# A 7x7 convolution beside attention: rows by six products for four outputs in place of four for two

## The chip, the cores and the metric

The program runs on one core of a Trainium2 chip. The metric is the device time of one execution in microseconds (us). The core has TensorE (PE, with its weight loads PEld), VectorE (DVE), ScalarE (ACT) and GpSimd (POOL) for the work, and SyncE (SP), whose queue issues the DMAs.

## The reference

There are three stages over four images x of 128 channels and 64x64 points. Only the first is touched here, called layer 0:

```python
def _L0_conv_ref(x, w7, b7, w5, b5, w3, b3, gw, gb, tw, tb, pw, pb, ow, ob):
    x7 = conv2d(x, w7, b7, 3)
    x5 = conv2d(x, w5, b5, 2)
    x3 = conv2d(x, w3, b3, 1)
    xn = nonlocal_block(x, gw, gb, tw, tb, pw, pb, ow, ob)
    return jax.nn.relu(x7 + x5 + x3 + xn + x)
...
x = x + _L0_conv_ref(_gn(x), ...)
```

`_gn` is a group norm. The three convolutions have the same input, so they are one 7x7 convolution with the summed kernel, 128 channels to 128. `nonlocal_block` is softmax attention over the 4096 points of an image, with 64-wide theta, phi and g, an output projection and a residual. Then follow a two-way selective state-space layer (`mamba`) and a recurrence over time (`recurrence`), both over the same `t`.

## The kernel before

All four images lie in SBUF as `t`, 128 channels by 4 x 4096. Layer 0 goes in 32 steps, eight per image. Each step does the attention of one block of 512 queries and one part of the convolution. The order of PE's instructions is the order of the code; on the other engines a scheduler orders them when the program is built, and each engine then keeps that order.

The attention of a step (`scores`, `values`): 16 times, two matmuls of 512 columns give scores `pf` in PSUM (two buffers), ACT takes the exponential `ex` (four buffers, L393), two matmuls multiply by `gT` and add to `acc`, and DVE sums the exponentials into `es` (L408). `divide` inverts the sums; `finish` projects.

The convolution divides the seven kernel rows into rows 0 to 2, row 3 and rows 4 to 6. Rows go by four products for two outputs (m = 0 to 3), and the two groups of three rows by three products in place of four (n = 0, 1, 2: both groups' sum, then each). Columns are treated the same way (kx = 0 to 3). An image is cut into two bands of 32 rows, held as the padded copies `xps[0]` and `xps[1]`; the four steps of a band are m = 1, 2, 0, 3. Per step:

- `forms(p, m)`: POOL makes `yx` (a combination of two rows, one buffer), `yd` (its differences, one buffer), and from them the column combinations `yf` (four buffers), each four instructions of 272 elements per partition.
- `convolve(p, i)`: for each n SP loads 576 KB of weights `wt` (two buffers) from `wd` in DRAM, and `products` makes 10 matmuls of 256 columns, or 20 where m is 0 or 3 and n is 1 or 2 (kernel row 3 with weights `wc` joins). An ACT copy (L348) and DVE additions bring PSUM into `eo`, POOL adds the n = 0 result (L358). m = 1 is kept as `mid`, m = 2 makes sum and difference with it, and m = 0 and 3 write the band's result `cv` (L372, POOL).

A band's `finish` comes in the first step of the next band: a matmul, an addition into `cv`, Relu with the bias (ACT, L426), and the addition to `t` (POOL, L428). In an image's last step `keys` makes the next image's `phi` and `gT` between the products, and `rows` normalises rows into `xps`. `weights` runs once at the start: it uses the places of images 1 to 3 in `t`, makes the column weights by `thirds` (L447 to L451), then 12 sets of `wd`, with a scaling by -1 on ACT (L467):

```python
for m in ORDER:
    one, two = lots[0][m], lots[1][m]
    both = fm.tile([P, 9, P], F32, tag="wt", name="both")
    nc.gpsimd.tensor_tensor(both, one, two, ALU.add)
    nc.sync.dma_start(wd[3 * m], both)
    nc.sync.dma_start(wd[3 * m + 1], one)
    nc.scalar.mul(two, two, -1.0)
    nc.sync.dma_start(wd[3 * m + 2], two)
```

Images 1 to 3 are loaded after it (`load(n)`), and `statistics` reads each with eight bn_stats.

Of the kernel before, what the change touches and what calls it, by code (L numbers as in the profile page):

```python
# [10 lines left out]
F32 = mybir.dt.float32  # L11
# [5 lines left out]
P = 128  # L17
# [136 lines left out]
def conv_attention(nc, tc, k, a, t, B, H, W, flags, load, mem, loads):  # L154
# [11 lines left out]

    T = H * W
# [4 lines left out]
    QB = 4  # L172
    RB = QB * RW
    PR, PC = RB // 2, W // 2
    KB = PR // 4
# [3 lines left out]
    SLOT = ((0, 1, 7, 2), (4, 5, 8, 6))  # L179

    with ExitStack() as ctx:
# [11 lines left out]
        xps = [wp.tile([P, RB + 6, WP], F32, name=f"xp{i}") for i in range(2)]  # L193
# [13 lines left out]
        for xp in xps:  # L207
            nc.gpsimd.memset(xp, 0.0)
# [3 lines left out]
        wd = [dram.tile([P, 9, P], F32, name=f"wd{i}") for i in range(12)]  # L212
# [60 lines left out]
        def rows(b, p):  # L273

            xp = xps[p % 2]
            first = 3 if p == 0 else 6
            n = min(RB + 6 - first, H - (p * RB + first - 3))
            if p == 0:
                nc.gpsimd.memset(xp[:, 0:3, :], 0.0)
            else:  # L280
                nc.vector.tensor_copy(xp[:, 0:6, :], xps[1 - p % 2][:, RB : RB + 6, :])
            nc.vector.tensor_scalar(
                xp[:, first : first + n, 3 : 3 + W],
                t[:, ds(b * T + (p * RB + first - 3) * W, n * W)].rearrange("p (h w) -> p h w", w=W),
                *gn[b], ALU.subtract, ALU.mult,
            )
            if first + n < RB + 6:
                nc.gpsimd.memset(xp[:, first + n :, :], 0.0)

        def combine(out, at, i):  # L290

            x, y, op = ((0, 2, ALU.subtract), (1, 2, ALU.add), (2, 1, ALU.subtract), (3, 1, ALU.subtract))[i]
            nc.gpsimd.tensor_tensor(out, at(x), at(y), op)  # L293

        def forms(p, m):

            xp = xps[p % 2]  # L300
            yx = fm.tile([P, PR + 2, WP], F32, tag="yx", name="yx", bufs=1)
            combine(yx, lambda j: xp[:, j : j + 2 * PR + 3 : 2, :], m)
            yd = fm.tile([P, PR, WP], F32, tag="yd", name="yd", bufs=1)

            def both(rows, g):
                v = rows.rearrange("p (k g e) c -> p k g e c", g=2, e=2)[:, :, g]
                f = fm.tile([P, 4, KB, 2, PC + 2], F32, tag="yf", name="yf", bufs=4)
                for kx in range(4):
                    combine(f[:, kx], lambda j: v[:, :, :, j : j + 2 * PC + 3 : 2], kx)
                return v, f  # L310

            out = [[both(yx[:, 0:PR], 1)]]
            nc.gpsimd.tensor_tensor(yd, yx[:, 0:PR], yx[:, 2 : PR + 2], ALU.subtract)
            for g in range(2):
                out.append([both(yd, g)])
                if m in (0, 3):
                    out[-1].append(both(xp[:, 3 + m // 3 : 3 + m // 3 + 2 * PR - 1 : 2, :], g))
            return out

        def products(f, kxs):  # L320

            pm = ps_c.tile([P, 2, PR * PC // 2], F32, tag="c", name="pm")
            for e, kx in enumerate(kxs):
                terms = []
                for rows, sums, wt in f:
                    for s in range(2):
                        terms.append((sums[:, kx, :, :, 2 * s : 2 * s + PC], wt[:, SLOT[s][kx], :]))
                    if kx in (0, 3):
                        c = 3 + kx // 3
                        terms.append((rows[:, :, :, c : c + 2 * PC - 1 : 2], wt[:, 3, :]))  # L330
                for i, (src, wt) in enumerate(terms):
                    nc.tensor.matmul(pm[:, e, :], wt, src, start=(i == 0), stop=(i == len(terms) - 1))  # L332
            return pm

        ORDER = (1, 2, 0, 3)

        def convolve(p, i):

            m = ORDER[i]
            base = None  # L340
            for n in range(3):
                wt = fm.tile([P, 9, P], F32, tag="wt", name="wt")
                nc.sync.dma_start(wt, wd[3 * m + n])
                f = [v + (u,) for v, u in zip(fs[p, m][n], (wt, wc))]
                pm = products(f, (1, 2))
                keep = n and m == 1
                eo = wk.tile([P, 2, PR * PC // 2], F32, tag=f"mid{n}" if keep else "eo", name="eo", bufs=1 if keep else 4)
                nc.scalar.copy(eo[:, 1, :], pm[:, 1, :])  # L348
                for e, op in enumerate((ALU.add, ALU.subtract)):
                    nc.vector.tensor_tensor(eo[:, e, :], pm[:, 0, :], eo[:, 1, :], op)  # L350
                yield
                pm = products(f, (0, 3))
                nc.vector.tensor_tensor(eo, eo, pm, ALU.add)  # L353
                if n == 0:
                    base = eo
                    yield
                    continue
                nc.gpsimd.tensor_tensor(eo, eo, base, ALU.add)  # L358
                if m == 1:
                    mid[n] = eo  # L360
                elif m == 2:
                    u = wk.tile([P, 2, PR * PC // 2], F32, tag=f"u{n}", name="u", bufs=1)
                    nc.gpsimd.tensor_tensor(u, mid[n], eo, ALU.add)
                    nc.gpsimd.tensor_tensor(mid[n], mid[n], eo, ALU.subtract)
                    mid[n] = [u, mid[n]]
                else:
                    if m == 0 and n == 1:
                        cv[p] = wk.tile([P, RB, W], F32, tag="cv", name="cv", bufs=1)
                    out = cv[p].rearrange("p (k g e q) (c x) -> p g q x k e c", g=2, e=2, q=2, x=2)[:, n - 1, m // 3]
                    in_ = lambda v: v.rearrange("p x (k e c) -> p x k e c", e=2, c=PC)  # L370
                    for x in range(2):
                        nc.gpsimd.tensor_tensor(out[:, x], in_(mid[n][m // 3])[:, x], in_(eo)[:, x], ALU.add)  # L372
                yield
            fs.pop((p, m))

        def queries(n):
            b, q = divmod(n, NQ)
            pt = ps_c.tile([P, NC], F32, tag="c", name="pt")
            r = 3 + (q % QB) * RW
            nc.tensor.matmul(pt, tw, xps[q // QB % 2][:, r : r + RW, 3 : 3 + W], start=True, stop=True)  # L380
# [29 lines left out]
        def divide(n, acc, es):  # L410
            den = ps_c.tile([P, NC], F32, tag="c", name="den")
            nc.tensor.matmul(den, k.ones, es[:, 0, :], start=True, stop=True)
            att = wk.tile([P, NC], F32, tag="att", name="att", bufs=QB + 1)
# [6 lines left out]
        def finish(n, att):  # L420
            b, q = divmod(n, NQ)
            pc = ps_c.tile([P, NC], F32, tag="c", name="pc")
            nc.tensor.matmul(pc, ow, att, start=True, stop=True)
            r = cv[n // QB][:, ds(q % QB * RW, RW), :].rearrange("p r c -> p (r c)")
            nc.vector.tensor_tensor(r, r, pc, ALU.add)
            nc.scalar.activation(r, r, AF.Relu, bias=bsum)  # L426
            tg = t[:, ds(n * NC, NC)]
            nc.gpsimd.tensor_tensor(tg, tg, r, ALU.add)  # L428

        def weights():  # L430
# [24 lines left out]
            lots = []  # L455
            for i, y in enumerate((0, 4)):
                new = free[:, 9 * (i + 1) : 9 * (i + 2), :]
                thirds([w[:, y + i] for i in range(3)], new)
                lots.append([w[:, y], w[:, y + 1], new, w[:, y + 2]])
            for m in ORDER:  # L460
                one, two = lots[0][m], lots[1][m]
                both = fm.tile([P, 9, P], F32, tag="wt", name="both")
                nc.gpsimd.tensor_tensor(both, one, two, ALU.add)
                nc.sync.dma_start(wd[3 * m], both)
                nc.sync.dma_start(wd[3 * m + 1], one)

                nc.scalar.mul(two, two, -1.0)  # L467
                nc.sync.dma_start(wd[3 * m + 2], two)
# [3 lines left out]
        gn, fs, mid, cv, atts = {}, {}, {}, {}, {}  # L472
        NB = NT // 4
        N = B * NQ
        gn[0] = statistics(0)
        rows(0, 0)
        th = None
        for j in range(T // XT):
# [4 lines left out]
            run(part)  # L483
        nxt = scores(th, 0)
        fm = ctx.enter_context(tc.tile_pool(name="l0_fm", bufs=2))
        weights()
        loads()
        for n in range(N):
            b, q = divmod(n, NQ)
            more = b + 1 < B and q == NQ - 1  # L490
            if 0 < n < B:
                load(n)
            m = ORDER[q % QB]
            fs[n // QB, m] = forms(q // QB, m)
            if b + 1 < B and q == NQ - 3:
                gn[b + 1] = statistics(b + 1)
            if (q + 1) % QB == 0 and n + 1 < N:
                rows(*divmod(n // QB + 1, NQ // QB))
# [9 lines left out]
            for i, _ in enumerate(convolve(n // QB, q % QB)):  # L508
                if i == 0:
                    if q % QB == 0 and n:  # L510
                        for m in range(n - QB, n):
                            finish(m, atts.pop(m))
                        cv.pop(n // QB - 1)
                    atts[n] = divide(n, acc, es)
                if more and i < T // XT:
# [9 lines left out]
                if more and i < T // XT:  # L525
                    run(part)
            if n + 1 < N:
                nxt = scores(th, 0)
        for m in range(N - QB, N):
            finish(m, atts.pop(m))  # L530
# [1066 lines left out]
```

## Time and profile before

| | us |
|---|---|
| three runs, median (lowest to highest) | 3230.27 (3229.05 to 3232.55) |
| the profiled execution, its span | 3233.0 |
| first product of the convolution (`pm`, L332) starts | 86.8 |
| last product of the convolution ends | 1733.7 |
| waits of PE's scores `pf` for ACT's `ex` up to 1740 | 28.5 |

The page gives an engine's busy time as a sum, then its busy share in 40 slices of the span (each digit is tenths), and groups of instructions with count, busy time and mean duration in ns of one, then the idle time before them and who ended it. A matmul in float32 stands as two records. In the timeline, the time in brackets is the engine's idle time before the row and its releaser.

### The profile page before, as it was taken

How to read it: one execution, taken by the hardware profiler on the slowest of the kernel's cores; microseconds unless marked ns; L12 is line 12 of the kernel's file. 1: busy time of each engine (PE TensorE's matmuls, PEld its weight loads, DVE VectorE, ACT ScalarE, POOL GpSimd, SP SyncE). 2: the span in 40 equal slices, each digit the busy share in tenths (PEclk: the TensorE clock that was granted, in tenths of full speed). 3: DMA queues.
4: the chain of work that ended last, by engine and by line, in shares of the span. 5: the costliest groups of instructions: out<-in, count | busy, mean ns of one | idle time of the engine just before them, and what ended most of it. 6: DMA issues, size and time to landing. Idle time of an engine off the chain costs nothing.

```text
span 3233.0 us, 43827 instructions
## 1 busy us (share of the span) xinstructions
PE 3043.7 (94%) x15991; PEld 1554.8 (48%) x15991; DVE 2140.1 (66%) x3431; ACT 1751.5 (54%) x3027; POOL 1796.9 (56%) x1487
## 2 busy tenths in 40 slices
PE   5999999999999999999997899999999999999986
PEld 1454544554545444545454354444444544444545
DVE  6865657667566566565664676767667767677667
ACT  3333333333333333342432787887788778888756
POOL 6565554845465546465472266556655665555554
PEclk8999999999999999999998899999999999999988
DMA  4301100101011010101011334333333343334332
GB/s 171 150 30 37 37 30 30 37 31 36 30 37 37 30 44 23 33 34 44 23 45 58 89 93 118 95 92 92 111 94 101 84 117 92 98 99 96 86 113 106
DMA packets 107245, 226.44 MB, mean 70 GB/s; under 512 B 25550, under 2 KB 29262, under 8 KB 105868
## 3 DMA queue, kind: packets, MB, share of 16 engines
q1 hardware_dynamic: 105804, 222.23, 23.4%
q8 instruction: 128, 2.10, 0.3%
q10 hardware_dynamic: 1216, 1.31, 0.1%
q14 instruction: 97, 0.79, 0.1%
HBM read 206.60 MB, written 16.90 MB: 69 GB/s over the span
## 4 chain that ended last, share of the span: by engine, by line
PE 78%; DVE 6%; POOL 5%; ACT 5%; DMA 3%; issue 2%; SPq 0%; POOLq 0%; ACTq 0%; DVEq 0%
PE pm L332 18%; PE acc L402 14%; PE pf L391 14%; PE pb L946 6%; PE px L958 3%; PE y L1077 3%; PE px L967 2%; PE acc L1419 2%; PE po L1148 2%; PE y L1085 2%; PE ptr L1020 2%; PE small L1055 2%; PE small L1032 1%; PE pm L1125 1%; DMA ct<-csmem 1%
## 5 line engine op out<-in xcount | busy, mean ns | idle before, releaser
L393 ACT ACTIVATE ex<-pf 128x1024 f32<-128x1024 f32 x512 | 496.7, 1021 | 515.8 <-PE pf L391 499.6
L408 DVE TENSOR_TENSOR es<-es,ex 128x1024 f32<-128x1024 f32 x448 | 626.3, 1398 | 160.1 <-ACT ex L393 129.1
L391 PE MATMUL pf<-theta,phi 64*128 64x512 f32 x2048 | 515.1, 622 | 28.9 <-ACT ex L393 28.5
L402 PE MATMUL acc<-ex,gT 128*64 128x512 f32 x2048 | 490.5, 605 | 0.0
L1045 POOL TENSOR_TENSOR ct<-ct,Cst 128x512 f32<-128x512 f32 x128 | 168.4, 1316 | 405.5 <-DMA ct<-csmem 348.4
L332 PE MATMUL pm<-yf,wt 128*128 128x256 f32 x1536 | 384.0, 380 | 0.0
L391 PEld LDWEIGHTS pf<-theta,phi 64*128 64x128 f32 x2048 | 174.6, 187 | 347.1 <-ACT ex L393 226.6
L332 PEld LDWEIGHTS pm<-yf,wt 128*128 128x128 f32 x1536 | 285.7, 189 | 95.3 <-issue 50.9
L1011 ACT ACTIVATE lt<-lt,cs 128x128 f32<-128x128 f32 x1024 | 312.1, 390 | 0.0
L293 POOL TENSOR_TENSOR yf<-yd 128x272 f32<-128x272 f32 x256 | 302.7, 1210 | 1.3
L348 ACT COPY eo<-pm 128x256 f32<-128x256 f32 x96 | 35.7, 372 | 480.3 <-PE pm L332 480.3
L402 PEld LDWEIGHTS acc<-ex,gT 128*64 128x64 f32 x2048 | 127.5, 136 | 337.7 <-issue 328.5
L293 POOL TENSOR_TENSOR yf<-xp 128x272 f32<-128x272 f32 x128 | 141.8, 1133 | 203.2 <-PE pm L332 203.2
L946 PE MATMUL pb<-tl,wbc_fwd 128*64 128x512 f32 x512 | 238.5, 609 | 2.7 <-DVE xT L978 2.5
L946 PE MATMUL pb<-tl,wbc_bwd 128*64 128x512 f32 x512 | 239.1, 609 | 0.0
L293 POOL TENSOR_TENSOR yx<-xp 128x1260 f32<-128x1260 f32 x32 | 84.6, 2645 | 215.5 <-PE pm L332 212.7
L350 DVE TENSOR_TENSOR eo<-pm,eo 128x256 f32<-128x256 f32 x192 | 80.7, 420 | 170.0 <-ACT eo L348 167.3
L353 DVE TENSOR_TENSOR eo<-eo,pm 128x512 f32<-128x512 f32 x96 | 64.2, 669 | 190.5 <-PE pm L332 190.1
L1110 POOL TENSOR_TENSOR yT<-yT,zT 128x512 f32<-128x512 f32 x127 | 168.2, 1333 | 37.9 <-DVE yT L1097 32.7
L1044 DVE TENSOR_TENSOR lt<-lt,gm 128x1024 f32<-128x1024 f32 x128 | 181.3, 1417 | 1.9
L1077 PE MATMUL y<-lt,xdt 128*64 128x128 f32 x2048 | 143.2, 283 | 6.7 <-PE ptr L1020 3.8
L978 DVE SCALAR_TENSOR_TENSOR xT<-px,taps_bwd,xT 128x512 f32<-128x512 f32 x192 | 143.7, 749 | 8.2 <-ACT xT L972 3.3
(274 smaller groups left out, 5607.4 us busy)
## 6 DMA issues: line engine op xcount, KB each, us to landing
lt<-csmem SPq DMA_DIRECT2D x128, 512.0 KB, 5.6
wt<-wd SPq DMA_DIRECT2D x96, 576.0 KB, 3.7
ct<-csmem SPq DMA_DIRECT2D x256, 128.0 KB, 5.3
rs<-m SPq DMA_DIRECT2D x31, 512.0 KB, 3.5
t<-in_x SPq DMA_DIRECT2D x4, 2048.0 KB, 9.4
rows<-after SPq DMA_DIRECT2D x32, 256.0 KB, 4.7
out<-t SPq DMA_DIRECT2D x4, 2048.0 KB, 14.3
tl<-scale SPq DMA_DIRECT2D x24, 256.0 KB, 5.4
```

The source lines that it names most:

```text
L293: nc.gpsimd.tensor_tensor(out, at(x), at(y), op)
L332: nc.tensor.matmul(pm[:, e, :], wt, src, start=(i == 0), stop=(i == len(terms) - 1))
L391: nc.tensor.matmul(pf[:, e, :], phi[HALF[e], m, :], th[HALF[e]], start=True, stop=True)
L393: nc.scalar.activation(ex, pf, AF.Exp, scale=scale)
L402: nc.tensor.matmul(acc[HALF[e]], gT[:, 2 * m + e, :], ex[:, e, :], start=(m == 0), stop=(m == NT // 2 - 1))
L408: nc.vector.tensor_tensor(es, es, ex, ALU.add)
L946: nc.tensor.matmul(out, w[i]["bc"][:, tap, bass.ts(c, DS)], src, start=(tap == 0), stop=(tap == KC - 1),)
L1011: nc.scalar.activation(v, v, AF.Relu, scale=-1.0, bias=m["b"]["cs"][:, d, m["i"], h : h + 1])
L1044: nc.vector.tensor_tensor(lt, lt, gm.unsqueeze(2).to_broadcast([P, ND, NHEAD, P]), ALU.mult)
L1045: nc.gpsimd.tensor_tensor(m["ct"], m["ct"], Cs[:, cols].unsqueeze(1).to_broadcast([P, NHEAD, P]), ALU.mult)
L1077: nc.tensor.matmul(y[HALF[h], d, c, at[d]], m["dt"][:, d, 2 * c + h, :], m["lt"][:, d, 2 * c + h, :], start=(i % 2 == 0 and c == 0), stop= ...
L1110: eng.tensor_tensor(v, v, gr["z"][d][:, :, half(d, j // 2)], ALU.mult)
```

## The change

Rows now go by six products for four outputs, at the points 0, 3/4, 3/2 and their negatives, with row 3's two middle outputs done by themselves (m = 6, 7, weights `wc`). The whole image is one padded copy `xp`, in blocks of four rows; its eight steps are m = 1, 2, 0, 6, 7, 5, 3, 4, in the last image 1, 2, 3, 4, 6, 7, 5, 0. `transform` replaces the one combination of rows by scalings on ACT and additions on POOL, into `yx` and `yb` that have one buffer each. The result is summed in the image's own place in `t`, and the input is read again from DRAM (`xr`) for the last addition, at the first step of the next image. `weights` makes 18 sets, in three parts: before step 0, in step 1 and in step 2; the loads of images 1 to 3 come after that. The core of the diff:

```diff
-            yx = fm.tile([P, PR + 2, WP], F32, tag="yx", name="yx", bufs=1)
-            combine(yx, lambda j: xp[:, j : j + 2 * PR + 3 : 2, :], m)
+            if m in (0, 5):
+                j = m // 5
+                nc.scalar.mul(yx, row(j + 2), -(UU + VV))
+                nc.scalar.mul(yb, row(j), UU * VV)
+                nc.gpsimd.tensor_tensor(yx, yx, row(j + 4), ALU.add)
+                nc.gpsimd.tensor_tensor(yx, yx, yb, ALU.add)
+            elif m in (1, 3):
+                nc.scalar.mul(yb, row(1), -(VV if m == 1 else UU))
+                nc.gpsimd.tensor_tensor(yb, yb, row(3), ALU.add)
+                nc.scalar.mul(yx, row(2), -(VV if m == 1 else UU))
+                nc.gpsimd.tensor_tensor(yx, yx, row(4), ALU.add)
+                nc.scalar.mul(yb, yb, U if m == 1 else V)
+                nc.gpsimd.tensor_tensor(yx, yx, yb, ALU.add)
+            else:
+                nc.scalar.mul(yb, yb, -2.0)
+                nc.gpsimd.tensor_tensor(yx, yx, yb, ALU.add)
...
+            if m >= 6:
+                return [None] + [[both(every(m - 2, KB), g)] for g in range(2)]
...
-                if m == 1:
+                if keep:
                     mid[n] = eo
                 elif m == 2:
-                    u = wk.tile([P, 2, PR * PC // 2], F32, tag=f"u{n}", name="u", bufs=1)
+                    nc.gpsimd.tensor_tensor(out(0), in_(mid[n]), in_(eo), ALU.add)
+                    nc.gpsimd.tensor_tensor(mid[n], mid[n], eo, ALU.subtract)
+                    nc.scalar.mul(out(2), out(0), UU)
+                    nc.scalar.mul(out(1), in_(mid[n]), U)
+                    nc.scalar.mul(out(3), in_(mid[n]), U * UU)
+                elif m == 4:
+                    u = wk.tile([P, 2, KB // 2 * PC], F32, tag="u", name="u", bufs=2)
                     nc.gpsimd.tensor_tensor(u, mid[n], eo, ALU.add)
                     nc.gpsimd.tensor_tensor(mid[n], mid[n], eo, ALU.subtract)
-                    mid[n] = [u, mid[n]]
+                    nc.gpsimd.tensor_tensor(out(0), out(0), in_(u), ALU.add)
+                    for j, v, by in ((2, u, VV), (1, mid[n], V), (3, mid[n], V * VV)):
+                        for x in range(2):
+                            nc.vector.scalar_tensor_tensor(
+                                out(j)[:, x], in_(v)[:, x], by, out(j)[:, x], ALU.mult, ALU.add
+                            )
                 else:
...
+                    j = {0: 0, 5: 3, 6: 1, 7: 2}[m]
+                    nc.gpsimd.tensor_tensor(out(j), out(j), in_(eo), ALU.add)
...
+        def finish(b):
+            for q in range(NQ):
+                xr = wk.tile([P, NC], F32, tag="xr", name="xr")
+                nc.sync.dma_start(xr, image_in(b)[:, bass.ts(q, NC)])
+                r = t[:, ds(b * T + q * NC, NC)]
+                nc.scalar.activation(r, r, AF.Relu, bias=bsum)
+                nc.gpsimd.tensor_tensor(r, r, xr, ALU.add)
...
+                for g, e, s, f in ((one, slot[1], by, slot[2]), (two, slot[3], -by, first)):
+                    nc.scalar.mul(odd, g[:, 1], s * at)
+                    nc.scalar.mul(e, g[:, 2], s * at * at)
+                    nc.vector.scalar_tensor_tensor(e, g[:, 0], s, e, ALU.mult, ALU.add)
+                    nc.gpsimd.tensor_tensor(f, e, odd, ALU.add)
+                    nc.gpsimd.tensor_tensor(e, e, odd, ALU.subtract)
+                    made.append((f, e))
+                for i, v in enumerate((odd, second)):
+                    nc.gpsimd.tensor_tensor(v, made[0][i], made[1][i], ALU.subtract)
...
+            pair(1, U, 0.5 / (UU * (UU - VV)))
+            yield
+            single(0, 0, 1.0 / (UU * VV))
+            yield
+            single(5, 2, 1.0)
+            pair(3, V, 0.5 / (VV * (VV - UU)))
+            yield
...
-            if 0 < n < B:
-                load(n)
+            if n in (1, 2):
+                next(making)
+            if 3 <= n < B + 2:
+                load(n - 2)
...
+                rows(b + 1, 0, H)
```

## The prediction

> **What bounds the kernel now.** Read first: the page's busy shares and slices.
>
> ```profile
> PE 3043.7 (94%) x15991; PEld 1554.8 (48%) x15991; DVE 2140.1 (66%) x3431; ACT 1751.5 (54%) x3027; POOL 1796.9 (56%) x1487
> PE   5999999999999999999997899999999999999986
> PEclk8999999999999999999998899999999999999988
> ```
>
> Layer 0 is slices 0 to 21 (its last product ends at 1733.7 us); only this part changes. After slice 0 TensorE is full at full clock. Next, stage windows over two steps, m=2 and m=0 (columns: window, length, busy us of PE, PEld, DVE, ACT, POOL with counts, clock, DMA share, GB/s):
>
> ```profile
> 525.60:571.75 46.15, 45.83 (x198) 21.78 (x197) 31.77 (x38) 17.32 (x20) 24.66 (x19) 1.00 0.11 39
> 571.75:626.60 54.85, 54.59 (x239) 29.33 (x238) 35.65 (x38) 17.31 (x20) 40.12 (x33) 1.00 0.10 35
> ```
>
> PE is busy 99%, the rest at most 73%. So removed products are worth their full time, unless a wait appears. The groups give prices:
>
> ```profile
> L332 PE MATMUL pm<-yf,wt 128*128 128x256 f32 x1536 | 384.0, 380 | 0.0
> L293 POOL TENSOR_TENSOR yf<-yx 128x272 f32<-128x272 f32 x128 | 79.6, 653 | 66.1 <-PE pm L332 64.8
> L293 POOL TENSOR_TENSOR yx<-xp 128x1260 f32<-128x1260 f32 x32 | 84.6, 2645 | 215.5 <-PE pm L332 212.7
> L313 POOL TENSOR_TENSOR yd<-yx 128x1120 f32<-128x1120 f32 x32 | 83.4, 2606 | 84.1 <-PE pm L332 84.1
> L358 POOL TENSOR_TENSOR eo<-eo 128x512 f32<-128x512 f32 x64 | 98.1, 1533 | 23.0 <-DVE eo L353 22.4
> ```
>
> Last, the timeline of the start: how ACT's own queue can starve PE.
>
> ```profile
> 60.60 1.02 ACT L393 ACTIVATE ex<-pf 128x1024 f32<-128x1024 f32 x1 [0.67 <-PE pf L391]
> 69.93 1.16 ACT L467 ACTIVATE t<-t 128x1152 f32<-128x1152 f32 x1 [8.30 <-POOL both L463]
> 73.48 1.16 ACT L467 ACTIVATE t<-t 128x1152 f32<-128x1152 f32 x1 [2.39 <-POOL both L463]
> 74.55 1.92 ACT L393 ACTIVATE ex<-pf 128x1024 f32<-128x1024 f32 x2
> ```
> ```profile
> 75.61 3.79 PE L391 MATMUL pf<-theta,phi 64*128 64x512 f32 x8 [8.50 <-ACT ex L393]
> 81.23 1.99 PE L391 MATMUL pf<-theta,phi 64*128 64x512 f32 x8
> ```
>
> A small scaling (L467) waits for POOL; the exponentials behind it stand still, so does PE for 8.5 us, and its next matmuls take 3.79 us, not 1.99, in a cold clock. After the start no ACT instruction of layer 0 waits for POOL.
>
> **The Trainium skill.** "TensorE: Matmul & The Clock Gate", section "Architectural detail: the array is 16× 32×32, not 1× 128×128": ACT and DVE queues are strict FIFO; the lines above agree. Its Part 1: a window of about 3.4 us without work halves PE's clock; agrees (3.79 against 1.99). "GPSIMD Engine Reference", "Key points": POOL shares its SBUF interfaces with VectorE and is slowed by two-input DVE work; agrees: `yf` takes 0.65 us alone, 1.6 beside the `es` adds. "VectorE: DVE Perf Modes", the errata section, prices an ACT instruction at (224+N)/1.2 ns: 1.2 us for the new 1190-element ones (an estimate; the trace has 1.16 for 1152).
>
> **The change part by part.**
> *Products.* Per image: before 2 bands x (30+30+50+50) = 320 matmuls of 256 columns; now 4x30 + 2x50 + 2x20 = 260. Over four images 240 fewer. In the chain 92 records (two per matmul) take 20.22 us: 0.44 each. 240 x 0.44 = **106 us** off the path. The other matmuls stay.
> *POOL.* Per image 104 `yf` for 128; 12 transform adds and 6 `yd` for 8 `yx` and 8 `yd`. The total stays near 60%: no bound, hidden in sum. What counts is its latency, since ACT now waits for it in three places: the scalings of `transform`, the scalings of m=2 into `t`, the Relus of `finish`. In the order that the built program gives each engine these stand ahead of exponentials; behind a waiting ACT instruction queue the next exponentials, and for those PE's scores (two `pf` buffers) and DVE's sums wait. I walk through each place with POOL's prices alone: 2.3 (1190 wide, from 2.39 for 1260), 2.6 (`yd`), 0.65 (`yf`), 1.3 (512 wide), 1.4 (512 into strided `t`, as two L372). POOL runs alone there, since DVE's sums wait too; that is the value taken.
>
> *m=2, every image.* Zero is when products n=0 end and `yx` is free for the next step's form. ACT scales `yx`: 1.3 (after PE). POOL's queue: two transform adds 6.0, four `yf` 8.5, `eo`+base (n=1) 9.8, `out(0)` 11.2, `mid` minus `eo` 12.5, `yd` 15.1, `eo`+base (n=2) 16.4, one `yf` 17.0, `out(0)` 18.4, one `yf` 19.1, subtraction 20.4. ACT's queue: three scalings for n=1, first exponential, three for n=2, second exponential: it ends at about 22.9, against 13.2 if nothing waited (PE ends the step at 10.1, then two score groups). **10 us**, for images 1 to 3: **30**.
> *Image boundary.* Seven Relus of `finish` stand behind only two exponentials and need the last additions of m=4: after PE's last product DVE's `eo` add, then POOL `yd` 2.7, `eo` 4.0, `yf`, `u` 5.9, `yf`, subtraction 7.9, `out(0)` 9.5; DVE's six multiply-adds (0.45 each, half of a 512-wide row at 0.75) end at 9.7. Third exponential 12.2 for 4.4; four more Relus of 0.72 before the fifth; PE reaches the third value group 7.9 late. Three boundaries: **24**. SP's queue is not the wait: `xr` loads stand ahead of the n=2 weights, but the eighth add clears 5.5 us into the next n=0, when that weight buffer is not yet free (6.1).
> *Last image, m=4.* Its DVE multiply-adds stand before the `es` sums and end at 24.7, the sums free `ex` late: **8**.
> *Smaller.* `yb` x 0.75 or 1.5 behind the whole-image `rows` (4096 wide, about 4.7 us from 2240 in 2.6) 2.4 per image; `yb` x -2 amid `keys` 2.3 per image: **14** over three.
> *Start.* Before, POOL begins the weights (L440) at 37.1. Now the transform's three adds, each waiting for an ACT scaling, come first: forms end at 46 to 49, so `thirds` starts 9 to 12 us later, though the four `both` of 3.2 us that followed it are gone from before step 0. In their place `pair` is six POOL instructions of 1152 (2.7 alone, 3.5 beside DVE), and the ACT scalings of `single`, ahead of the last six exponentials, wait for their end and for the weight writes (3.1 us): the 16th exponential ends at 94 to 99, the first product starts at 95 to 101, against 86.8. I take 97, nearer the price of POOL alone: **10**. Step 1's first exponential waits behind `pair`'s scaling: **4**. Step 2: the second `pair` puts four 2.7 us instructions into the m=2 chain above, so the second exponential comes 20 late. SP issues the three image loads (9.4 us each) only behind the last weight write and two weight loads; the 24 bn_stats that read them (0.67 each) stand in DVE's queue among this step's 15 `es` sums (1.35 each), so that DVE needs 36 us where PE needs 26: **20 + 10**. Before, these loads left at 83.8 to 102.3 and cost nothing.
> *Cold clock.* Seven gaps over 5 us, 1.9 each at most: **10**.
> *End.* Relu and last add on 1024-wide pieces, already collected: 7 us after the last product for 10: **3** gained.
> Losses 30+24+8+14+10+4+30+10 = 130; gains 109. 3233 + 21 = 3254 in this execution's span; the three timed runs (3229.05 to 3232.55) have a median 3 lower: **3252**. ACT and POOL sums are unmeasured in this order: for each wait the lower bound is zero (the queue is read wrongly or filled elsewhere), the upper half as much again (POOL at its contended prices).
>
> **Rivals.** (1) The matmuls rule: PE stays near full, POOL's latency is largely absorbed. For it: PE at 99%, POOL at 53 to 73% per step. Against: strict queues and the 8.5 us gap shown. With the steady waits at a third (76 becomes 25), the start at 35, cold clock 4: 3230-109+64 = 3185 to 3215. (2) Balance: waits near 109 us, 0.84 of mine: 3224 to 3237, within 0.2% of before. (3) My forecast: the ACT-waits-for-POOL chain costs more than the products save; it decides from 109 us of waits on. (4) POOL runs at contended prices throughout (`eo` 2.25, `yf` 1.6, pairs 3.5): waits half larger, 3290 to 3310. That the change does not remove products can be excluded: the built program has 240 fewer.
>
> **How the numbers follow.** Slower (3 and 4) 0.62, same (2) 0.10, faster (1) 0.28. 0.2% (6.5 us) is about what a measurement of this kernel can tell from no change. Range 3190 to 3300: it takes in most of rival 1 and half of rival 4; the slower case's own range is 3237 to 3300.
>
> **What would show it.** Right: `pm` near 1040 matmuls (2080 records); waits of PE `pf` for ACT `ex` above 80 us (28.5 before), ACT's scalings and Relus waiting for POOL about 10 us at each m=2 step and 8 at each boundary; first product at 94 to 101. Wrong: steps following m=2 lasting as long as their products ask, PE busy 99% from 300 us on, or the loss lying in SP's weight loads.

## The result and the profile after

| | before | changed |
|---|---|---|
| median, us (lowest to highest, 4 runs each) | 3231.38 (3229.05 to 3232.55) | 3261.61 (3257.25 to 3263.97) |
| profiled span, us | 3233.0 | 3261.3 |
| first and last product of layer 0, us | 86.8, 1733.7 | 100.7, 1772.0 |
| convolution matmuls (two records each) | 1280 | 1040 |

The ratio is 1.0093, 95% interval 1.0075 to 1.011: slower. The page of the changed kernel, the lines that answer to those of before, and behind them the kernel before's line for the scores:

```profile
PE 2971.3 (91%) x15511; PEld 1471.5 (45%) x15511; DVE 2143.3 (66%) x3450; ACT 1818.7 (56%) x3093; POOL 1624.1 (50%) x1352
...
PE   5879998899988999899898899999999999999986
...
PEclk8889999999999999999998899999999999999988
...
L421 PE MATMUL pf<-theta,phi 64*128 64x512 f32 x2048 | 536.2, 643 | 115.4 <-ACT ex L423 115.4
```
```profile
L391 PE MATMUL pf<-theta,phi 64*128 64x512 f32 x2048 | 515.1, 622 | 28.9 <-ACT ex L393 28.5
```

PE has 480 records fewer (two per matmul) and is 72 us less busy, yet the span is 28 longer: the slices of layer 0 that were full now hold eights. The lines of the scores name the wait: over the whole span they stand 115.4 us for ACT's exponentials, where they stood 28.5; from 80 us to the end of layer 0 it is 101.1 against 12.6. No engine is full. A step with m=2, from one `den` matmul to the next (columns as in the windows above):

```profile
595.13:655.36 60.23, 50.97 (x202) 23.10 (x200) 31.25 (x41) 23.55 (x29) 28.46 (x26) 0.89 0.09 30
```

PE is busy 85% where it had 99%, the other engines between 38% and 52%, and the clock is at 0.89. What ACT waited for in layer 0 (its waits for POOL and DVE between 80 and 1800 us, the longest among them: total, times, longest):

```profile
...
ACT t L388 <- POOL t L386: 35.3, 8, 8.8
ACT yb L309 <- POOL yx L306: 30.4, 7, 6.2
ACT t L461 <- DVE t L398: 27.5, 3, 10.7
...
ACT ex L423 <- DVE es L436: 18.5, 2, 13.7
...
ACT yb L305 <- POOL yb L302: 18.0, 7, 3.3
...
ACT t L527 <- POOL t L521: 8.1, 1, 8.1
```

L388 is a scaling of m=2, L461 a Relu of `finish`, L305 and L309 scalings of `yb`, L527 a weight scaling at the start. Exponentials stand behind each. Which of these waits cost TensorE time is not in this list; that needs steps and experiments. The table takes the time from each step's `den` matmul to the next, in us, read from PE's timeline: the row of step n holds the products after `den` n-1 and the attention of step n. Steps count from 0, eight to an image.

| steps | what is in them | before | changed |
|---|---|---|---|
| up to step 0's `den` | start, weights | 88.6 | 103.7 |
| 1, 2, 3 | first m=1, m=2, m=0 | 45.6 + 45.6 + 54.4 | 52.1 + 74.0 + 57.6 |
| 9 to 16 | image 1's `den` to image 2's | 426.4 | 426.0 |
| 17 to 24 | image 2's to image 3's | 424.4 | 423.8 |
| 25 to 31 | image 3, up to its last `den` | 349.4 | 350.5 |
| last `den` to the end | | 1520.5 | 1511.5 |

So two full images take just as long as before: what 60 fewer products save is lost inside each image. The net loss is the first image (step 8's `den` at 549.5 against 512.3), 37 us, less 9 after the last `den`. Of these 9, 8 come behind the last addition of layer 0, in stages that no run touches and that differ by up to 9 us among the traces that have the same code there.

### The profile page after: what moved, and what is told of

The parts are those of the page before. It is cut to its first block, busy times and chain, and to the rows that moved or that the text cites. A ratio compares the mean times of both kernels' runs of the same rounds, so it can differ in the third digit from the quotient of the medians.

```text
span 3261.3 us, 42819 instructions
## 1 busy us (share of the span) xinstructions
PE 2971.3 (91%) x15511; PEld 1471.5 (45%) x15511; DVE 2143.3 (66%) x3450; ACT 1818.7 (56%) x3093; POOL 1624.1 (50%) x1352
## 5 line engine op out<-in xcount | busy, mean ns | idle before, releaser
L438 DVE TENSOR_TENSOR es<-es,ex 128x1024 f32<-128x1024 f32 x448 | 607.9, 1357 | 219.5 <-ACT ex L423 190.9
L421 PE MATMUL pf<-theta,phi 64*128 64x512 f32 x2048 | 536.2, 643 | 115.4 <-ACT ex L423 115.4
L432 PE MATMUL acc<-ex,gT 128*64 128x512 f32 x2048 | 501.5, 616 | 0.7 <-ACT ex L423 0.7
L325 POOL TENSOR_TENSOR yf<-xp 128x272 f32<-128x272 f32 x128 | 101.3, 821 | 398.9 <-PE pm L351 398.9
L351 PE MATMUL pm<-yf,wt 128*128 128x256 f32 x1152 | 287.8, 382 | 0.1
L351 PEld LDWEIGHTS pm<-yf,wt 128*128 128x128 f32 x1152 | 213.9, 190 | 73.2 <-issue 41.3
L325 POOL TENSOR_TENSOR yf<-yd 128x272 f32<-128x272 f32 x192 | 189.5, 1015 | 13.0 <-PE pm L351 12.6
L371 DVE TENSOR_TENSOR eo<-pm,eo 128x256 f32<-128x256 f32 x176 | 73.8, 419 | 179.1 <-ACT eo L369 176.9
L1029 PEld LDWEIGHTS pb<-tl,wbc_fwd 128*64 128x64 f32 x512 | 65.9, 139 | 165.8 <-issue 138.7
L1147 POOL TENSOR_TENSOR S<-S,tot 128x256 f32<-128x256 f32 x120 | 93.2, 776 | 92.5 <-PE y L1168 87.8
```

Of the source, the lines that this page charges most:

```text
L325: nc.gpsimd.tensor_tensor(f[:, kx], at(x), at(y), op)
L421: nc.tensor.matmul(pf[:, e, :], phi[HALF[e], m, :], th[HALF[e]], start=True, stop=True)
L432: nc.tensor.matmul(acc[HALF[e]], gT[:, 2 * m + e, :], ex[:, e, :], start=(m == 0), stop=(m == NT // 2 - 1))
L438: nc.vector.tensor_tensor(es, es, ex, ALU.add)
L1029: nc.tensor.matmul(out, w[i]["bc"][:, tap, bass.ts(c, DS)], src, start=(tap == 0), stop=(tap == KC - 1),)
```

## The experiments

Times are medians; the kernel before had 3231 to 3234 beside them. "The changed kernel" is 3261.6.

**The products alone.** Edit, in the kernel before:

```diff
-                pm = products(f, (1, 2))
+                pm = products(f, (1, 2), n)   # the same for (0, 3)
...
+                if n:
+                    terms.pop()
```

> The kernel before, with 256 of its 2560 convolution matmuls left out (the last term of every sum in n=1 and n=2), so the output is not the reference's. Theory (a matmul of 256 columns is worth 0.44 us because TensorE is the bound): 256 x 0.44 = 113 us less, 3231 becomes 3115 to 3122. Rival (the products are partly hidden, some other engine follows close behind): 40 to 80 us less.

(The 2560 counts records: 256 of 1280 matmuls were left out.) Measured 3150.5 (ratio 0.974, 0.9723 to 0.9757): 83 less, between the two. Most steps, with 8 matmuls fewer each, are 2.8 to 3.6 us shorter, 0.35 to 0.45 a matmul, so the price is right there. Of the 30 us that are missing, more than half came back as waits, even without any new instruction on ACT: between 80 us and the last `den` PE stood idle 41.5 us in place of 24.0. The last step of images 0 to 2 became 1.0 to 2.4 us longer, and PE's waits for `ex` rose from 12.6 to 26.3, in places like this one (PE's timeline; the bracket is the idle time ahead and what ended it):

```profile
404.26 3.47 PE L393 MATMUL pf<-theta,phi 64*128 64x512 f32 x8 [4.44 <-ACT ex L395]
```

**The scalings of m=2.** Edit, three lines like this:

```diff
-                    nc.scalar.mul(out(2), out(0), UU)
+                    nc.gpsimd.tensor_scalar(out(2), out(0), UU, None, ALU.mult)
```

> The changed kernel with the six scalings of m=2 moved from ScalarE to GpSimd, so that no ScalarE instruction of that step waits for GpSimd's sums; six more GpSimd instructions per image. Theory (exponentials queue behind these scalings): the 46.4 us of attention in the m=2 steps of images 1 to 3 fall to 33 to 36, step 2 gains some 5 to 10, in all 35 to 50 us less than the changed kernel: 3212 to 3227. Rival (TensorE waits there because GpSimd has too much to do, whoever scales): no gain or a loss, 3255 to 3275.

Measured 3223.7 (0.9966, 0.9955 to 0.9978): 38 less, the theory, and already below the kernel before. The steps in question fell from 60.2, 59.6, 59.7 to 47.8, 47.3, 47.3; step 2 hardly moved (74.0 to 72.8). In the changed kernel, step 9 to 10, ACT's timeline, and PE's beside it:

```profile
610.63 0.67 ACT L388 ACTIVATE t<-t 128x512 f32<-128x512 f32 x1 [3.92 <-POOL t L386]
...
613.10 0.99 ACT L423 ACTIVATE ex<-pf 128x1024 f32<-128x1024 f32 x1
618.15 0.66 ACT L388 ACTIVATE t<-t 128x512 f32<-128x512 f32 x1 [4.07 <-POOL t L386]
619.98 0.67 ACT L389 ACTIVATE t<-eo 128x512 f32<-128x512 f32 x1 [1.17 <-POOL eo L387]
620.55 0.64 ACT L390 ACTIVATE t<-eo 128x512 f32<-128x512 f32 x1
621.09 1.91 ACT L423 ACTIVATE ex<-pf 128x1024 f32<-128x1024 f32 x2
```
```profile
614.14 2.08 PE L421 MATMUL pf<-theta,phi 64*128 64x512 f32 x4 [3.33 <-ACT ex L423]
622.14 2.08 PE L421 MATMUL pf<-theta,phi 64*128 64x512 f32 x4 [5.92 <-ACT ex L423]
624.15 3.31 PE L432 MATMUL acc<-ex,gT 128*64 128x512 f32 x8
```

GpSimd's timeline with the scalings moved:

```profile
610.64 1.60 POOL L388 TENSOR_SCALAR t<-t 128x512 f32<-128x512 f32 x1
612.31 1.54 POOL L389 TENSOR_SCALAR t<-eo 128x512 f32<-128x512 f32 x1
613.91 1.54 POOL L390 TENSOR_SCALAR t<-eo 128x512 f32<-128x512 f32 x1
```

On ACT the second exponential comes 8 us after the first, and PE stands 3.33 and 5.92 us. On GpSimd each scaling costs 1.5 to 2.7 us in place of 0.66, and no exponential is behind it.

**The boundary: Relus or multiply-adds?** The prediction put the boundaries (steps 8, 16, 24) on the Relus, and the last image's m=4 (step 28) on DVE's multiply-adds ahead of the `es` sums. But the boundaries have these additions too. Two single edits: the additions to GpSimd, and the Relus one step later.

```diff
-                        for x in range(2):
-                            nc.vector.scalar_tensor_tensor(
-                                out(j)[:, x], in_(v)[:, x], by, out(j)[:, x], ALU.mult, ALU.add
-                            )
...
+                        nc.gpsimd.tensor_scalar(w, v, by, None, ALU.mult)
+                        nc.gpsimd.tensor_tensor(out(j), out(j), in_(w), ALU.add)
```

> The changed kernel with the multiply-adds of m=4 (six per group, twelve per image) moved from VectorE to GpSimd as a scaling and an add each. Theory A (the Relus of finish are what stops ScalarE at the image boundaries, VectorE's multiply-adds stop only the last image's m=4): the last image's 12.7 us go, but at the boundaries the Relus now wait for GpSimd's longer chain and lose 3 to 10 us more each: in all 3255 to 3285. Theory B (VectorE's multiply-adds ahead of the es sums are what stops the boundaries too): boundaries shorter as well, 3225 to 3245.

```diff
+            nc.vector.scalar_tensor_tensor(bs, att[:, 0:1], 0.0, bsum, ALU.mult, ALU.add)
...
-                nc.scalar.activation(r, r, AF.Relu, bias=bsum)
+                nc.scalar.activation(r, r, AF.Relu, bias=bs)
```

> The changed kernel with the Relus of finish held back by one step: their bias is bsum plus zero times the attention of step 1 of the next image, so they cannot stand at the boundary. Theory A (the Relus are the boundary's stop): the three boundaries lose 8 to 11 us less each, 3230 to 3238. Theory B (VectorE's multiply-adds would stop the es sums there anyway, as they do in the last image, where no Relu is near): 0 to 9 us less in all, 3252 to 3262.

Measured 3293.8 and 3273.4: both slower than the changed kernel and outside both their expectations. With the additions on GpSimd the boundaries grew by 12 to 13 us each, and step 28 fell by 12.4, of which step 29 gave 6.8 back. With the Relus late the boundaries fell by only 3.5 to 3.8 each, and the eight Relus, now in one row ahead of m=2's scalings, lengthened steps 10, 18 and 26 by 7. So the Relus were 3.5 to 3.8 us of a loss of 8 to 11 (the next runs give its size). The rest is DVE's: with the Relus out of the way, an exponential of the boundary stands 7.79 us for DVE's sums, almost as long as the 8.4 us that the first Relu stood there for the additions. The line is ACT's in the run with late Relus; below it is DVE's timeline in the changed kernel:

```profile
519.21 1.94 ACT L423 ACTIVATE ex<-pf 128x1024 f32<-128x1024 f32 x2 [7.79 <-DVE es L436]
```
```profile
511.89 2.26 DVE L398 SCALAR_TENSOR_TENSOR t<-u,t 128x256 f32<-128x256 f32 x2 [3.69 <-POOL u L393]
514.08 3.86 DVE L398 SCALAR_TENSOR_TENSOR t<-eo,t 128x256 f32<-128x256 f32 x4
517.86 1.67 DVE L436 TENSOR_TENSOR es<-ex 128x1024 f32<-128x1024 f32 x1
```

The first `es` sum of the step cannot start before 517.86, and four `ex` buffers are soon full. At 0.86 us (from `eo`) and 1.04 us (from `u`) in the mean the additions also took twice the 0.45 that the prediction gave them.

**Both spread out.** The additions two at a time behind the `es` sums, the Relus one at a time among the exponentials; then the additions alone.

```diff
+                if i and late:
...
+                    nc.vector.scalar_tensor_tensor(kv, exs[1][:, 0, 0:3], 0.0, by, ALU.mult, ALU.add)
+                    for _ in range(2):
+                        o, v, c = late.pop(0)
+                        nc.vector.scalar_tensor_tensor(o, v, kv[:, c : c + 1], o, ALU.mult, ALU.add)
+                if q == 1 and b:
+                    finish(b - 1, i, exs[1])   # one Relu, bias bsum + 0 * ex, made by DVE
```

> The changed kernel with the multiply-adds of m=4 spread over the attention of the following step, two behind every second es sum, and the Relus of finish spread likewise over step 1 of the next image (their factors and bias take in zero times an exponential of that moment, which fixes the place); layer statistics of image 0 begin one step later. Same work on the same engines. Theory B (at the boundaries and at the last image's m=4 it is VectorE's multiply-adds, waiting for GpSimd ahead of the es sums, that stop the exponentials): the 32 us of the boundaries and 12.7 of the last m=4 go but for 1 to 3 us each, 35 to 42 less: 3219 to 3227. Rival (these steps are short of VectorE time, so 12 multiply-adds cost the same wherever they stand): 0 to 12 less, 3250 to 3262.

> The changed kernel with only the multiply-adds of m=4 spread over the following step's attention; the Relus of finish are as in the changed kernel and follow those additions and the last collect by their data alone. Theory (at the boundary ScalarE and VectorE both stood behind the multiply-adds; the 6.9 us that the spread Relus then cost in step 1 of each image came from their bias made by VectorE, a ring from exponential to es sum to bias to Relus to exponential): boundaries 8 to 11 shorter, last m=4 8 shorter, step 1 of an image unchanged: 30 to 40 less than 3261.6, 3222 to 3232. Rival (Relus cost 7 us per image wherever they stand): 3240 to 3248, as with both spread.

Measured 3245.2 (1.0036, 1.0022 to 1.005) and 3260.5 (1.0079, 1.0064 to 1.0095). Neither theory held as put. The boundaries did fall to 62.8 (8.1 to 11.2 less each) and step 28 to 51.1 (8.0 less), as theory B said, but with both spread the next step (9, 17, 25) grew by 6.8 to 6.9. With the additions alone the boundaries were 68.3, 68.3 and 68.2: the Relus, free to go once the additions were done, stood ahead of the exponentials there (the first Relu stood 6.9 us for the last addition), and again 7 us each appeared in the next step: a scaling of `yb`, behind GpSimd's additions to the Relus' results, came no earlier than in the changed kernel (555.5 against 556.0), `theta` comes behind it on ACT, so PE waited 3.6 us for `theta`, and its next six matmuls took 5.5 us where they had taken 2.75. The spread Relus show the ring in its barest form, ACT and DVE side by side:

```profile
569.02 0.72 ACT L460 ACTIVATE t<-t,bs 128x512 f32<-128x512 f32 x1 [3.11 <-DVE bs L456]
569.64 1.92 ACT L421 ACTIVATE ex<-pf 128x1024 f32<-128x1024 f32 x2
```
```profile
570.68 3.58 DVE L436 TENSOR_TENSOR es<-es,ex 128x1024 f32<-128x1024 f32 x2 [1.70 <-ACT ex L421]
574.18 0.15 DVE L456 SCALAR_TENSOR_TENSOR bs<-ex,bsum 128x1 f32<-128x1 f32 x1
576.03 2.81 DVE L436 TENSOR_TENSOR es<-es,ex 128x1024 f32<-128x1024 f32 x2 [1.70 <-ACT ex L421]
```

The bias takes 0.15 us, but it stands behind two sums; the Relu waits for it, two exponentials wait for the Relu, the next sums wait for these. ACT stood 16.9 us in that step with both engines far from full.

**The start and step 2.** The second `pair` tied to the end of step 2, or the loads of images 2 and 3 tied to steps 10 and 18:

```diff
+            nc.vector.tensor_scalar(scale, atts[after][:, 0:1], 0.0, s * at, ALU.mult, ALU.add)
-            nc.scalar.mul(odd, g[:, 1], s * at)
+            nc.scalar.mul(odd, g[:, 1], scale)
```

> The changed kernel with the second pair of weight products tied to the end of step 2's attention, so that its GpSimd work and its ScalarE scalings fall in step 3; the image loads follow one step later. Theory (it delays step 2's m=2 chain on GpSimd): step 2's attention, 60.8 us, falls to 43 to 50 and step 3 pays 0 to 6: 5 to 17 less, 3245 to 3257. Rival (the statistics and loads set step 2's length, and move along to step 3 with the same price): 3258 to 3265.

```diff
-            if 3 <= n < B + 2:
-                load(n - 2)
+            if n in LOADS:                     # (3, 10, 18)
+                i = LOADS.index(n) + 1
+                nc.vector.tensor_copy(t[:, i * T : i * T + 1], atts[n - 1][:, 0:1])
+                load(i)
```

> The changed kernel with the loads of images 2 and 3 tied to steps 10 and 18, so that their 16 bn_stats no longer stand among step 2's es sums. Theory (VectorE is overfull in step 2): 16 x 0.68 = 11 us less VectorE work there, step 2 shorter by 5 to 10: 3251 to 3257. Rival (those sums fall into time in which VectorE waits anyway): 3259 to 3263.

The later pair measured 3263.5: nothing. Steps 1 and 2 fell by 6.4 and 15.1, step 3 grew by 21.8. The cost of the pair with loads and statistics went along with them. The loads apart measured 3254.3 (1.0065, 1.0048 to 1.0082), 7.3 less than the changed kernel: step 2 fell by 7.5 and step 3 by 2.2, as the theory had it.

**All of it.** All these moves together, and the second scaling of `yb` on GpSimd:

```diff
-                nc.scalar.mul(yb, yb, -2.0)
+                nc.gpsimd.tensor_scalar(yb, yb, -2.0, None, ALU.mult)   # U and V likewise
```

> The changed kernel with all of these moves: m=2 scalings and the second scaling of yb on GpSimd, multiply-adds of m=4 and Relus spread, second pair one step later, image loads apart. If the losses are independent queue waits: 38 (m=2) + 35 to 42 (spread) + 8 to 12 (yb) + 10 to 17 (pair and loads) less than 3261.6: 3153 to 3171, below both kernels by over 60. Rival (GpSimd, with more work and in the same chains, becomes the wait): 3185 to 3215.

Measured 3183.6 (0.9852, 0.9836 to 0.9869): below both kernels, but short of the sum. The trace had the reason: steps 9, 17 and 25 still had their 7 to 9 us. Making the bias on ACT breaks that ring:

```diff
-            nc.vector.scalar_tensor_tensor(bs, ex[:, 0, 0:1], 0.0, bsum, ALU.mult, ALU.add)
+            nc.scalar.activation(bs, ex[:, 0, 0:1], AF.Identity, bias=bsum, scale=0.0)
```

> All moves, with the bias of each spread Relu made by ScalarE itself in place of VectorE, so that no Relu waits for VectorE's queue. Theory (the ring of waits): step 1 of images 1 to 3 falls from 52.5 to 54.6 us to 46 to 48, three times 6 to 7 us: 3163 to 3168. Rival (ScalarE has no room for eight Relus there): 3178 to 3186.

Measured **3162.6** (0.9781, 0.9766 to 0.9796): steps 9, 17, 25 at 47.2, 47.9, 47.1. Its page, and its wait for exponentials from 80 to 1740 us (the changed kernel had 101.1):

```profile
PE   4899999999999999999996999999999999999986
...
PEclk8999999999999999999997999999999999999988
```
```profile
PE pf L419 <- ACT ex L421: 20.5, 33, 6.7
```

The slices are full again with 240 matmuls fewer. Two tries at the start on top of it, each by itself: the scalings of `single` tied to later steps, and the last two subtractions of the first pair on DVE:

```diff
-                nc.scalar.mul(v[0], one[:, i], by)
...
+                    nc.vector.tensor_scalar(scale, atts[after][:, 0:1], 0.0, s, ALU.mult, ALU.add)
+                    nc.scalar.mul(u, g[:, i], scale)   # both scalings
```

> The kernel of the run with all moves and ScalarE-made biases, with the weight scalings for m=0 and m=5 tied to the attention of steps 0 and 1, so that at the start they do not wait for GpSimd ahead of the first sixteen exponentials. Theory (this wait is most of the 9.7 us hole at 85 to 94 us, which moved the first product from 86.8 to over 100): first product 5 to 12 us earlier, 0 to 4 us given back in steps 1 and 2: 3152 to 3164, below the run without it by 3 to 12. Rival (the start waits for the pair's weights, which come no sooner): within 3 us of the run without it, or later.

```diff
-                    nc.gpsimd.tensor_tensor(v, made[0][i], made[1][i], ALU.subtract)
+                    (nc.gpsimd if after else nc.vector).tensor_tensor(v, made[0][i], made[1][i], ALU.subtract)
```

> All moves with ScalarE-made biases, and the two last subtractions of the first weight pair (1152 wide, 3.5 and 2.6 us on GpSimd) on VectorE. Theory (the start waits for GpSimd's six additions of the first pair, one after the other, and a scaling behind them holds the exponentials): these two leave the chain, the first product (105.9 without it) comes 3 to 6 us earlier, 3156 to 3160. Rival (VectorE's es sums there wait for the same pair instead, or the start waits for the transform that GpSimd does ahead of the weights): first product within 2 us, 3161 to 3166.

The first measured 3164.1: its rival. The first product came 1.4 us earlier (104.5 for 105.9), and step 2 grew by 7.3 (the stages behind layer 0 were 4.5 us shorter in that execution, so the time alone shows less). The second measured 3159.3 (0.9769, 0.9754 to 0.9784); in the trace the first product starts 3.6 us earlier, at 102.3, with every later step as before within 2. The time alone cannot tell it from 3162.6. It is the fastest of all, 2.3% under the kernel before.

## Why the prediction was right

It forecast 3252 and slower; 3261.6 is inside the slower case's range. The mechanism, exponentials queued behind ACT instructions that wait for GpSimd, is shown for m=2 by the run that took those away; at the boundary it holds only in part, since DVE's queue stops the exponentials there too. The terms (a size taken from a run is what that run won back):

| term | forecast | measured | from |
|---|---|---|---|
| 240 products | 106 gained | 26.1 and 22.6 in the two full images, for 60 x 0.44 = 26.4 | all moves with ACT-made bias, against before |
| m=2, images 1 to 3 | 30 | 12.4 + 12.3 + 12.4 = 37 | m=2 scalings moved |
| image boundaries | 24, by the Relus | 8.1 + 11.2 + 8.2 = 27; Relus 3.5 to 3.8 each | both spread; Relus late |
| last m=4 | 8 | 12.4 in step 28, of which spreading won back 8.0 | m=4 additions on GpSimd; both spread |
| `yb` | 14 | 11, not taken alone in any run | all moves: steps 7, 15, 23 (3.8 together), boundaries 62.8 to 60.4 (7.1) |
| start | 10 | 13.9 (first product 100.7) | trace |
| step 1 | 4 | 6.4 | table; 45.7 with the pair late |
| step 2, and step 3 | 30, 0 | 26.7, 1.8 | all moves with ACT-made bias: step 2 at 47.3, step 11 for step 3 at 55.8 (in that run steps 3 and 4 themselves are 7.5 longer than in the changed kernel) |
| end | 3 gained | 9 gained, 8 of them behind layer 0; last product to last addition 10.0 before, 8.1 now | table; traces |

The losses measured add to 136 and the gains, with the products at their price, to 115: 21, where the profiled spans differ by 28. So about 7 us are in no row. The forecast had 21 too, from 130 and 109: m=2, the last m=4, the start and step 1 came out larger, and the cold clock, 10 by itself there, lies inside the rows here.

*Products.* Right where the waits are gone. Rival 1 took them for granted; the run with fewer products shows that even with no new instruction on ACT a quarter of the gain is lost, more than half of it (17.5 us) as idle time of PE.

*m=2.* The prediction's walk had the second exponential end at 22.9 us after the products of n=0; in step 9 to 10 it is 23.2. The measured 12.4 is more than 10 because the clock goes cold in the same place: PE stands 9.3 us, and the matmuls behind its two holes take about 3.4 more than warm ones (2.08, 2.08 and 3.31 us against about 1.05, 1.05 and 1.94). The prediction charged that in a term of its own (10); here it is inside each row.

*The boundary* is the step that failed in its cause: "Seven Relus of `finish` stand behind only two exponentials" is true, and holding them back won a third to a half of the loss; DVE's multiply-adds ahead of the `es` sums, which the prediction charged only in the last image and at 0.45 us each in place of 0.9 to 1.0, cost the rest. The two overlap: the additions spread alone shortened the boundaries by only 2.6 to 5.7. That the forecast of 24 came close to the 27 is therefore luck. Its list of what would show it (ACT's Relu waiting about 8 us) was met with 8.4 and did not tell the two apart, since both wait for the same additions.

*Step 2.* The size was near and both parts exist (bn_stats: 9.7 us in steps 2 and 3), but the run with a later pair shows that the cost goes where the pair goes.

*The start.* Forecast 10, measured 14. On top of all moves, GpSimd's subtractions of the first pair were worth 3.6 us; the scalings of `single` are not the cause. The transform's GpSimd work ahead of the weights was not taken away in any run, but all moves added to it, with two scalings of `yb`. GpSimd's first instruction for the weights, in the kernel before, the changed one and that with ACT-made bias:

```profile
37.13 2.62 POOL L440 TENSOR_TENSOR t<-t,wc 128x1152 f32<-128x1152 f32 x1
```
```profile
46.85 2.61 POOL L490 TENSOR_TENSOR t<-t,wc 128x1152 f32<-128x1152 f32 x1
```
```profile
53.02 2.60 POOL L489 TENSOR_TENSOR t<-t,wc 128x1152 f32<-128x1152 f32 x1
```

It comes 9.7 us later, as forecast, and then another 6.2; the first product starts at 86.8, 100.7 and 105.9. So this work does lie on the path to the first product; how much of the 14 it is alone stays open.

Rival 4 (waits half larger) is out: its sum would be 3290 or more, and in the m=2 step GpSimd's prices are mostly those without contention (512-wide additions at 1.27 us, most `yf` at 0.63 to 0.66).

## What to carry to other kernels

Before removing work from a full engine, list the instructions that each edit puts into another engine's queue ahead of what feeds that engine, and ask of each whom it waits for: six scalings of 0.66 us in the wrong queue cost as much as 28 matmuls of 0.44. Here moving them to the engine that makes their operand won, though they ran there at about a third of the speed (1.8 us in the mean). A wait that is moved, not broken, turns up in the next step, so read the time step by step, not from the total.

## What was not expected of the hardware

Over all traces of this case, in layer 0: holes of PE up to 2.4 us left the next eight records of the scores (four matmuls) at 2.0 us, but for two places with 2.8 and 3.0 us after 1.8 and 2.1. Holes of 3.3 us and more gave 3.3 to 4.0 us for eight; where only four records followed, they mostly took 2.08 us, but 1.1 to 2.0 in eight places, after 3.3 to 3.8. Between them it went either way: 2.05 us after 3.23, and 3.42 after 2.60. The Trainium skill ("TensorE: Matmul & The Clock Gate", Part 1) gives a window of about 3.4 us that runs freely, whenever the hole begins; an edge that is not sharp agrees with that, though the holes under 3.4 us that were followed by slow matmuls are not explained by it alone.

A GpSimd scaling of 512 elements took 1.5 to 2.7 us, one of 1190 elements 3.2 (once, at the start, 6.4), longer than an addition of two tensors of that size (2.5 to 2.7 in most places). A subtraction of 1152 elements took 1.36 us on DVE, 2.6 to 3.7 on GpSimd.
